# Moving the filter loads and the stores from SyncE to GpSimd, and four engines to written order, in an attention

## The chip, the cores and the metric

The kernel runs on one core of one Trainium2 chip. The metric is the device time of one execution in microseconds, the median of several runs. One further execution is recorded by the hardware profiler; its page and its trace are what the text below reads. The engines are TensorE (PE in the profile, PEld for its weight loads), VectorE (DVE), ScalarE (ACT), GpSimd (POOL) and SyncE (SP; SPq is the queue of transfers that it issues). Each engine works through its own list of instructions in order and waits on semaphores for the others.

## The reference

The input is an image batch of 2 x 128 channels x 64 x 64. Layer 0 is a convolution-attention block (a group norm, 7 x 7 neighbourhood attention, three small matrices and normalisations) added to the image. Layer 1 sees each image as 4096 tokens of 128 numbers:

```python
t = _to_tokens(x)
t = t + _L1_attn_ref(_ln_t(t))            # global attention, one head
t = t + _L1_ffn_ref(_ln_t(t), ...)        # sum of spectral filters

# _L1_attn_ref(q): queries, keys and values are the same tokens
sim = jnp.einsum('blh,bmh->blm', q, q) * scale
sim = jnp.where(diag[None, :, :], jnp.float32(-1000000000.0), sim)
attn = jax.nn.softmax(sim, axis=-1)
return jnp.einsum('blm,bmh->blh', attn, q)

# _compute_spectral: convolutions with 16 filters, then 128 x 128 matrices
out = jnp.einsum('btkd,k,kde->bte', U_plus, s, Mpp)
out = out + jnp.einsum('btkd,k,kde->bte', U_minus, s, Mpm)
```

The last part is done for four branches, each on a leading fraction of the tokens and with its own matrices, and the branches are added with weights that a softmax over `log_weights + gumbel` gives. Since a query is also a key, `sim` is symmetric.

## The kernel before

All arithmetic is in float32. The kernel has three stretches of time: layer 0 and the making of tokens (up to about 350 us, where its last work overlaps with the first attention), the global attention of image 0 and then of image 1 (about 350 to 1310 us), and the spectral filters as convolutions by matmul (from about 1310 us to the end), which the change leaves alone.

**Attention.** `attention(b, fill)` cuts 4096 tokens into 8 chunks of 512 and walks 36 pairs (a, c) with c >= a. A pair has four steps, each for 128 queries of chunk a. In a step, `weights` multiplies a query tile with the keys of chunk c into a PSUM bank (L927, near the diagonal L936), and ScalarE takes the exponential (L932, L943). The matmuls of a pair are issued while the pair before is used. The exponentials serve twice, because of the symmetry. Once as they are: `other` (L1049) adds up what chunk a gives to chunk c, in one PSUM buffer, which VectorE adds to the sums `xa` after the fourth step (L1066, L1068). And once turned, for what chunk c gives to chunk a (`own`, L983, in `onto`). To turn them, `sent` writes the pair's 1 MB to `eb` in HBM from ScalarE's queue (L956), `moved` reads it back with the partition groups exchanged in four transfers of 256 KB from SyncE's queue (L963, two buffers `et`), and `turned` transposes blocks of 32 x 32 on VectorE (L972, two instructions). Constants say how many steps after the sending each follows: `MOVE` 3 for the reads, `TURN` 7 for the transposes, `DELAY` 8 for the matmuls. `pass_on(2)` issues what has come due, at most two `own` products in a step.

**Fill.** After each step `fill()` advances generators, one piece of other work at a time. Urgent ones come first. `after(b, c)` takes a chunk that is complete: transposes (L1088), division by the softmax's sum (VectorE, L1091 to L1100), a layer norm (statistics L183, L184 on VectorE, the power -1/2 L174 on GpSimd, `z` L191 on VectorE), its transposes (L202) and copy (L1113), and short transforms of the tokens as matmuls (L1142, L1155). Their results are copied by ScalarE (`uo`, L1120), added and subtracted by `adder[0]`, which is GpSimd during the attentions (`ub`, L1123), and stored to `us` in HBM by SyncE (L1127, and in halves of 64 rows L1132). Behind the urgent ones stand, in attention 0, `filters()` (transforms of the spectral filters: matmuls L1325, sums on GpSimd L1337, L1348, stores of rows to `gs` by SyncE, L1312) and `tokens(1)`, the normalised tokens of image 1. In attention 1 there is `for_ffn`: `filter_matrices` mixes the 2 x 16 matrices of four branches in 8 groups of four (`mixed`: a load of 256 KB by SyncE, L1256, into the pool `st`, then GpSimd L1259, or L1263 and L1264), and after each pair of groups makes scaled sums and differences (L1276 to L1281); then blocks of convolution filters are loaded (`ct`, L1424).

**Order.** The instructions go to the engines through a scheduler, which may move an instruction ahead of others of its engine, except those marked `keep_in_program_order`: the reads in `moved` (L963), the transposes in `turned` (L972) and the matmuls in `onto` (L983) keep their order. Semaphores and buffers are worked out from the resulting order.

Of the kernel before, what the change touches and what calls it, by code (L numbers as in the profile page):

```python
# [24 lines left out]
MOVE, TURN, DELAY = 3, 7, 8  # L25
# [77 lines left out]
def kernel(  # L103
# [773 lines left out]
    with ap_:  # L877
# [24 lines left out]
        def attention(b, fill):  # L902
# [78 lines left out]
            def onto(own, n, out_, e, first, last):  # L981
                tc.keep_in_program_order(
                    nc.tensor.matmul(out_, lhsT=tok[b][:, n, :], rhs=e, start=first, stop=last, skip_group_check=True)  # L983
                )
# [22 lines left out]
            coming_, late, turns, owns = [], [], [], {}  # L1007
# [22 lines left out]

            es, halves = [], []
            for k in range(4):
                es.append(weights(0, 0, k, es, halves))
            for i, (a, c) in enumerate(pairs):
# [6 lines left out]
                for j in range(4):  # L1041
                    if following:
                        coming.append(coming_of(*following, j, coming, halves))
                    n = 4 * CHUNKS[a] + j
                    turn = lambda v, o: v.rearrange(o, q=4) if far(a, c) else v
                    if a == c:
# [11 lines left out]
                    pass_on(2)  # L1058
# [15 lines left out]
            complete(7, owns[7])  # L1074


        spare = [tok[0][:, 0:4, :]]
        adder = [nc.gpsimd]

        def after(b, c):  # L1080
# [35 lines left out]
            def store(pu, n, r0, m, ri):  # L1116

                for s in range(2):
# [5 lines left out]
                    for sgn in range(2):  # L1124
                        to = us[r0 : r0 + m, sgn, :, 2 * hh + s, 2 * fp : 2 * fp + 2, b, par, :]
                        if ri is not None:
                            nc.sync.dma_start(  # L1127
# [3 lines left out]
                        for f in range(2):  # L1131
                            nc.sync.dma_start(  # L1132
# [73 lines left out]
        def branch_weights():  # L1206
# [40 lines left out]
            for _ in mixed(mu, m_u, nc.vector, False):  # L1247
                pass
            yield

        def mixed(dst, src, eng, steps):
            dst2 = dst.rearrange("p k e -> p (k e)")
            for i in range(NBR):
                st = sp.tile([P, 4, P], F32, tag="st", name="st")
                n = src.shape[1]
                nc.sync.dma_start(out=st[:, 0:n], in_=src[i].rearrange("k d e -> d k e"))  # L1256
                st2 = st[:, 0:n].rearrange("p k e -> p (k e)")
                if i == 0:
                    eng.tensor_scalar(dst2, st2, wt[:, 0:1], None, ALU.mult)  # L1259
                elif eng is nc.vector:  # L1260
                    eng.scalar_tensor_tensor(dst2, st2, wt[:, i : i + 1], dst2, ALU.mult, ALU.add)
                else:
                    eng.tensor_scalar(st2, st2, wt[:, i : i + 1], None, ALU.mult)  # L1263
                    eng.tensor_tensor(dst2, dst2, st2, ALU.add)  # L1264
# [549 lines left out]
```

## Time and profile before

| what | value |
|---|---|
| time, median of 3 runs (lowest to highest) | 2090.71 us (2090.48 to 2095.21) |
| the profiled execution's own time | 2097.21 us |
| its span, first to last instruction | 2095.5 us |
| mean granted TensorE clock | 0.963 |
| TensorE busy | 1931.1 us (92%) |
| VectorE, ScalarE, GpSimd busy | 910.3, 723.4, 682.4 us |
| SyncE's reads of turned weights, `et` | 216 of 256 KB |
| SyncE's stores `us` from `ub`, of 128 KB | 128 |

The profile's page gives busy times, a picture of the span in 40 equal slices (a digit is the busy share in tenths, 52.4 us a slice), the chain of work that ended last, and groups of instructions by line, with their mean duration, the idle time of the engine just ahead of them and what ended it. Beyond the page, the trace answers for a window: the busy time of every engine, an engine's instructions in order of time, or what it waited for. A name such as `own L983 <- DVE et L972` reads: the instruction of line 983 that writes `own` waited for VectorE's instruction of line 972 that wrote `et`. Where lines of different kernels are named, they are lines of that kernel's own file.

### The profile page before, as it was taken

What the parts mean: (1) busy time and instruction counts of PE and PEld (TensorE: products, weight loads), DVE (VectorE), ACT (ScalarE), POOL (GpSimd) and SP (SyncE); (2) the same over time, 40 slices, a digit from 0 to 9 for tenths busy, and PEclk for the clock granted to TensorE, in tenths of its full rate; (3) what the DMA queues carried; (4) which work ended last, traced back from release to release, by engine and by line L of the source; (5) the groups of instructions that cost most, each with busy time, mean ns of one, the idle gap of its engine ahead of it and who ended that gap; (6) DMA issues with size and microseconds to landing.
All of it is one profiled execution on the core that took longest, in us unless ns stands there. A gap on an engine that the chain in (4) does not pass through costs nothing.

```text
span 2095.5 us, 51013 instructions
## 1 busy us (share of the span) xinstructions
PE 1931.1 (92%) x20504; PEld 1357.0 (65%) x20504; DVE 910.3 (43%) x2874; ACT 723.4 (35%) x1686; POOL 682.4 (33%) x1054
## 2 busy tenths in 40 slices
PE   6899998998899999995388998999999999999998
PEld 4677775444444444442133444699999899999987
DVE  5799986543433343422123335333333334333332
ACT  3789885313222234121022232222222222222222
POOL 4367976243011123028751111022222112222211
PEclk8999999999999999998689998999999999999999
DMA  4222222676466536466356641322222123222211
GB/s 150 62 61 61 62 60 65 199 184 187 137 191 180 164 86 214 122 184 171 101 155 167 185 134 52 87 67 66 68 66 64 46 58 100 66 70 67 66 45 42
DMA packets 278379, 225.98 MB, mean 108 GB/s; under 512 B 122607, under 2 KB 241535, under 8 KB 270720
## 3 DMA queue, kind: packets, MB, share of 16 engines
q1 hardware_dynamic: 269442, 162.59, 31.2%
q10 hardware_dynamic: 8126, 58.04, 7.0%
q8 instruction: 163, 2.67, 0.5%
q0 software_dynamic: 576, 2.10, 0.3%
q14 instruction: 72, 0.59, 0.1%
HBM read 131.40 MB, written 91.25 MB: 106 GB/s over the span
## 4 chain that ended last, share of the span: by engine, by line
PE 63%; issue 11%; POOL 9%; DMA 7%; DVE 6%; SPq 2%; ACT 1%; POOLq 0%; DVEq 0%; ACTq 0%
PE acc L1542 27%; PE pc L1523 7%; PE own L983 6%; PE bank L927 5%; PE other L1049 5%; PE bank L349 2%; PE bank L559 2%; POOL ub L1123 2%; PE bank L202 1%; POOL st L1263 1%; DMA et<-eb 1%; DMA st<-in_m_plus_dram 1%; DMA us<-ub 1%; PE bank L1142 1%; DMA st<-in_m_minus_dram 1%
## 5 line engine op out<-in xcount | busy, mean ns | idle before, releaser
L1528 DVE COPY y<-pc 128x512 f32<-128x512 f32 x320 | 206.1, 686 | 349.2 <-PE pc L1523 349.0
L1542 PE MATMUL acc<-y,mpl 32*128 32x256 f32 x5120 | 324.3, 379 | 0.8 <-DVE af L1552 0.8
L1542 PE MATMUL acc<-y,mmi 32*128 32x256 f32 x5120 | 316.5, 375 | 0.0
L1528 ACT COPY y<-pc 128x512 f32<-128x512 f32 x320 | 171.9, 589 | 397.5 <-PE pc L1523 392.9
L1542 PEld LDWEIGHTS acc<-y,mpl 32*128 32x128 f32 x5120 | 289.4, 186 | 8.0 <-DVE af L1552 1.3
L1542 PEld LDWEIGHTS acc<-y,mmi 32*128 32x128 f32 x5120 | 290.9, 185 | 3.9
L983 PE MATMUL own<-et,tok 128*128 128x512 f32 x448 | 217.3, 622 | 62.6 <-DVE et L972 60.8
L932 ACT ACTIVATE e<-bank 128x512 f32<-128x512 f32 x216 | 128.8, 599 | 406.7 <-PE bank L927 394.8
L1553 POOL TENSOR_TENSOR af<-af 128x512 f32<-128x512 f32 x39 | 49.7, 1274 | 591.8 <-DVE af L1552 540.2
L927 PE MATMUL bank<-cm 128*128 128x512 f32 x432 | 225.2, 612 | 4.5 <-ACT uo L1120 4.5
L1049 PE MATMUL other<-e,tok 128*128 128x512 f32 x448 | 225.2, 599 | 4.2 <-DVE xa L1066 4.2
L1523 PE MATMUL pc<-ct,ut 32*128 32x256 f32 x2560 | 214.5, 380 | 3.9 <-DMA ut<-us 2.1
L983 PEld LDWEIGHTS own<-et,tok 128*128 128x128 f32 x448 | 86.2, 199 | 175.4 <-issue 94.3
L1523 PEld LDWEIGHTS pc<-ct,ut 32*128 32x128 f32 x2560 | 174.4, 188 | 10.4 <-DVE y L1528 3.9
L972 DVE STREAM_TRANSPOSE et<-et 128x1024 f32<-128x1024 f32 x108 | 127.7, 1219 | 105.1 <-DMA et<-eb 105.1
L174 POOL TENSOR_TENSOR ln_rs<-ln_rs,mhalf 128x4 f32<-128x4 f32 x24 | 24.4, 1017 | 404.9 <-DVE ln_rs L173 404.9
L1049 PEld LDWEIGHTS other<-e,tok 128*128 128x128 f32 x448 | 82.8, 192 | 103.1 <-issue 95.4
L1123 POOL TENSOR_TENSOR ub<-uo 128x256 f32<-128x256 f32 (+1 forms) x164 | 99.8, 641 | 100.5 <-ACT uo L1120 69.5
L927 PEld LDWEIGHTS bank<-cm 128*128 128x128 f32 x432 | 76.7, 195 | 76.8 <-issue 62.1
L546 ACT ACTIVATE p<-p,mn 128x196 f32<-128x196 f32 x256 | 114.4, 449 | 14.1 <-DVE mn L536 13.6
L1066 DVE TENSOR_TENSOR xa<-other,xa 128x512 f32<-128x512 f32 x42 | 28.9, 687 | 167.9 <-PE other L1049 167.7
L536 DVE CUSTOM_DVE_ANT_0 p<-bank,tab 128x196 f32<-128x196 f32 x256 | 76.4, 353 | 4.9 <-PE bank L523 4.7
(262 smaller groups left out, 2607.1 us busy)
## 6 DMA issues: line engine op xcount, KB each, us to landing
eb<-e ACTq DMA_DIRECT2D x54, 1024.0 KB
et<-eb SPq DMA_DIRECT2D x216, 256.0 KB
ut<-us SPq DMA_DIRECT2D x160, 128.0 KB
us<-ub SPq DMA_DIRECT2D x128, 128.0 KB
ct<-gs SPq DMA_DIRECT2D x320, 40.0 KB
vw<-vd SPq DMA_DIRECT2D x256, 49.0 KB
ct<-gs SPq DMA_DIRECT2D x320, 32.0 KB
vd<-v SPq DMA_DIRECT2D x128, 32.0 KB
```

What stands on the lines that cost most here:

```text
L536: nc.vector.tensor_tensor_reduce(t[name + "p"][:, h, :], t[name + "S"][h][:, 0:KEYS], tab[:, ci, h, :], 1.0, 3.0e38, ALU.add, ALU.min, t[n ...
L546: nc.scalar.activation(p, p, AF.Exp, bias=t[name + "mn"][:, h : h + 1], scale=-1.0, accum_out=t["den"][:, u, h : h + 1],)
L927: nc.tensor.matmul(ps.rearrange("p (q t j) -> p q t j", q=4, t=4), lhsT=cm[b][:, n * P : (n + 1) * P], rhs=keys.rearrange("p (t q j) -> p ...
L932: nc.scalar.activation(e, ps.rearrange("p (q r) -> p q r", q=4), AF.Exp, bias=0.0, scale=ASCALE)
L972: tc.keep_in_program_order(nc.vector.transpose(flat, flat))
L983: nc.tensor.matmul(out_, lhsT=tok[b][:, n, :], rhs=e, start=first, stop=last, skip_group_check=True)
L1049: nc.tensor.matmul(turn(other, "p (q r) -> p q r"), lhsT=tok[b][:, n, :], rhs=es[j], start=(j == 0), stop=(j == 3),)
L1123: adder[0].tensor_tensor(ub[:, sgn, 0:n], both[:, 0:n], both[:, n : 2 * n], op)
L1523: nc.tensor.matmul(pcs[j].rearrange("p (g o c) -> p o g c", g=4, o=2)[:, :, at], lhsT=ut[rows_, par, :], rhs=cv_[rows_], start=True, stop= ...
L1528: (nc.scalar.copy if j % 2 else nc.vector.tensor_copy)(y[:, :, :, 4 * kl + j, :], pcs[j].rearrange("p (g x k) -> p k g x", g=4, k=KF))
L1542: nc.tensor.matmul(acc[j][:, 0:256], lhsT=(mmi if l else mpl)[rows_, k, :], rhs=y[rows_, k, 2 * l : 2 * l + 2].rearrange("p s n x -> p (s ...
L1553: eng.tensor_tensor(af[:, 0:2], af[:, 0:2], af[:, 2:4], ALU.add)
```

## The change

The change has two halves. Transfers: the loads of the branch matrices in `filter_matrices`, the stores of filter rows to `gs` and the stores of token transforms to `us` are issued by GpSimd in place of SyncE, the last until attention 1 has ended (`adder` gets a second entry for that). The loads come through a new function `branch`, one branch ahead of its mixing, and a fill now carries one branch rather than two, with the sums and differences in a fill of their own; the small matrices `mu` are mixed by VectorE as before and loaded by SyncE. `filters` hands over after every row of sums, not every second. What SyncE issues in the attentions is then the reads `et`, filter blocks `ct` and a few constants.

Order: from the step of attention 0 at which the buffer for image 1's tokens exists (`tt[1]`), and in all of attention 1, until each attention's end, a `manual_schedule` takes TensorE, VectorE, ScalarE and GpSimd out of the scheduler's hands: they run in the order in which the program writes them. SyncE stays with the scheduler. `onto` no longer has its own mark. `MOVE` goes from 3 to 2. At a pair's first step `pass_on(2)` comes ahead of the product `other`, at the other steps behind it as before. In attention 1 a `fill()` follows each of the first four weight products.

```diff
--- before.py
+++ after.py
@@ -22,7 +22,7 @@
 KF = 16
 NBR = 4
 MASKED = -1.0e30
-MOVE, TURN, DELAY = 3, 7, 8
+MOVE, TURN, DELAY = 2, 7, 8
 
 DIAG = -1.0e6
 QSCALE = DH ** -0.5
@@ -979,9 +979,7 @@
                 nc.vector.tensor_copy(et[:, m], pt)
 
             def onto(own, n, out_, e, first, last):
-                tc.keep_in_program_order(
-                    nc.tensor.matmul(out_, lhsT=tok[b][:, n, :], rhs=e, start=first, stop=last, skip_group_check=True)
-                )
+                nc.tensor.matmul(out_, lhsT=tok[b][:, n, :], rhs=e, start=first, stop=last, skip_group_check=True)
 
             def complete(a, own):
                 xs = xa[b][:, chunk(a)]
@@ -1004,7 +1002,7 @@
                 if (c, t) == (7, 3):
                     complete(a, own)
 
-            coming_, late, turns, owns = [], [], [], {}
+            coming_, late, turns, ordered, owns = [], [], [], [], {}
             step = 0
 
             def coming_of(a, c, k, left, halves):
@@ -1028,9 +1026,12 @@
                     pair_onto(owns[a], a, c, et, t)
                     n -= 1
 
+            written = ExitStack()
             es, halves = [], []
             for k in range(4):
                 es.append(weights(0, 0, k, es, halves))
+                if b:
+                    fill()
             for i, (a, c) in enumerate(pairs):
                 following = pairs[i + 1] if i + 1 < len(pairs) else None
                 coming, halves = [], []
@@ -1039,10 +1040,14 @@
                 else:
                     owns[a] = ps_o.tile([P, 512], F32, tag="own", name="own", bufs=2)
                 for j in range(4):
+                    if tt[1] is not None and not ordered:
+                        ordered.append(written.enter_context(tc.manual_schedule(engines={engines.PE, engines.DVE, engines.Activation, engines.Pool})))
                     if following:
                         coming.append(coming_of(*following, j, coming, halves))
                     n = 4 * CHUNKS[a] + j
                     turn = lambda v, o: v.rearrange(o, q=4) if far(a, c) else v
+                    if j == 0:
+                        pass_on(2)
                     if a == c:
                         onto(owns[a], n, owns[a], es[j], j == 0, a == 7 and j == 3)
                     else:
@@ -1055,7 +1060,8 @@
                             here = ep.tile([P, 4, 512], F32, tag="et", name="et", bufs=2)
                         turned_here(here, es, j)
                         late.append((step + 1, a, c, here, j))
-                    pass_on(2)
+                    if j:
+                        pass_on(2)
                     fill()
                     step += 1
                 if a != c:
@@ -1072,10 +1078,11 @@
                 pass_on(2)
                 fill()
             complete(7, owns[7])
+            written.close()
 
 
         spare = [tok[0][:, 0:4, :]]
-        adder = [nc.gpsimd]
+        adder = [nc.gpsimd, nc.gpsimd]
 
         def after(b, c):
 
@@ -1124,12 +1131,12 @@
                     for sgn in range(2):
                         to = us[r0 : r0 + m, sgn, :, 2 * hh + s, 2 * fp : 2 * fp + 2, b, par, :]
                         if ri is not None:
-                            nc.sync.dma_start(
+                            adder[1].dma_start(
                                 out=to[:, ri], in_=ub[:, sgn, :].rearrange("p (f d) -> p f d", d=P)
                             )
                             continue
                         for f in range(2):
-                            nc.sync.dma_start(
+                            adder[1].dma_start(
                                 out=to[:, :, f].rearrange("k i d -> i k d"), in_=ub[64 * f : 64 * f + 64, sgn, 0:P]
                             )
 
@@ -1244,33 +1251,37 @@
             nc.vector.tensor_tensor(wt, wt, ys, ALU.add)
 
             yield
-            for _ in mixed(mu, m_u, nc.vector, False):
-                pass
-            yield
-
-        def mixed(dst, src, eng, steps):
-            dst2 = dst.rearrange("p k e -> p (k e)")
+            mu2 = mu.rearrange("p k e -> p (k e)")
             for i in range(NBR):
-                st = sp.tile([P, 4, P], F32, tag="st", name="st")
-                n = src.shape[1]
-                nc.sync.dma_start(out=st[:, 0:n], in_=src[i].rearrange("k d e -> d k e"))
-                st2 = st[:, 0:n].rearrange("p k e -> p (k e)")
+                st = branch(m_u, i, nc.sync)
                 if i == 0:
-                    eng.tensor_scalar(dst2, st2, wt[:, 0:1], None, ALU.mult)
-                elif eng is nc.vector:
-                    eng.scalar_tensor_tensor(dst2, st2, wt[:, i : i + 1], dst2, ALU.mult, ALU.add)
+                    nc.vector.tensor_scalar(mu2, st, wt[:, 0:1], None, ALU.mult)
                 else:
-                    eng.tensor_scalar(st2, st2, wt[:, i : i + 1], None, ALU.mult)
-                    eng.tensor_tensor(dst2, dst2, st2, ALU.add)
-                if i % 2 and steps:
-                    yield
+                    nc.vector.scalar_tensor_tensor(mu2, st, wt[:, i : i + 1], mu2, ALU.mult, ALU.add)
+            yield
+
+        def branch(src, i, eng):
+
+            st = sp.tile([P, 4, P], F32, tag="st", name="st")[:, 0 : src.shape[1]]
+            eng.dma_start(out=st, in_=src[i].rearrange("k d e -> d k e"))
+            return st.rearrange("p k e -> p (k e)")
 
         def filter_matrices(mpl, mmi):
 
-            for k0 in range(0, KF, 4):
-                for dst, src in ((mpl, m_plus), (mmi, m_minus)):
-                    yield from mixed(dst[:, k0 : k0 + 4, :], src[:, k0 : k0 + 4], nc.gpsimd, True)
-
+            parts_ = [(k0, dst, src, i) for k0 in range(0, KF, 4) for dst, src in ((mpl, m_plus), (mmi, m_minus)) for i in range(NBR)]
+            loaded = [branch(m_plus[:, 0:4], 0, nc.gpsimd)]
+            for at, (k0, dst, src, i) in enumerate(parts_):
+                if at + 1 < len(parts_):
+                    k1, _, src1, i1 = parts_[at + 1]
+                    loaded.append(branch(src1[:, k1 : k1 + 4], i1, nc.gpsimd))
+                st = loaded.pop(0)
+                dst2 = dst[:, k0 : k0 + 4].rearrange("p k e -> p (k e)")
+                nc.gpsimd.tensor_scalar(dst2 if i == 0 else st, st, wt[:, i : i + 1], None, ALU.mult)
+                if i:
+                    nc.gpsimd.tensor_tensor(dst2, dst2, st, ALU.add)
+                yield
+                if dst is mpl or i + 1 < NBR:
+                    continue
                 a, d = (m[:, k0 : k0 + 4, :].rearrange("p k e -> p (k e)") for m in (mpl, mmi))
                 s = sp.tile([P, 512], F32, tag="st", name="mdiff")
                 nc.gpsimd.tensor_tensor(s, a, d, ALU.subtract)
@@ -1309,7 +1320,7 @@
                     gs.tensor, gs.offset + r0 * 4 * SG * GROW + (i * SG + s) * GROW + o * LL,
                     [[4 * SG * GROW, n], [2 * SG * GROW, 2], [1, LL]],
                 )
-                nc.sync.dma_start(out=to, in_=src)
+                nc.gpsimd.dma_start(out=to, in_=src)
 
             everything = [(r0, c0 + ri * P, (ri,), P) for r0, c0 in row_tiles for ri in range(2)]
             everything.append((left_row, left_col, (0, 1), 64))
@@ -1347,8 +1358,7 @@
                         fn = sp.tile([P, 2, LL], F32, tag="ub", name="fn", bufs=4)
                         nc.gpsimd.tensor_scalar(fn[mine], fb[mine], -1.0, None, ALU.mult)
                         store(fn[mine], r0, n, 1, s, 1, 0)
-                    if a == 1:
-                        yield
+                    yield
 
         def residual_of(lags):
             for _ in range(4):
@@ -1462,7 +1472,7 @@
         kept = []
         fill, left = filler(1, steps, kept)
         attention(1, fill)
-        adder[0] = nc.vector
+        adder[:] = nc.vector, nc.sync
         for gen in steps:
             for _ in gen:
                 pass
```

More of the change, by code (lines that the diff above doesn't have):

```diff
@@ L1246, in branch_weights @@
             yield
-            for _ in mixed(mu, m_u, nc.vector, False):
-                pass
-            yield
-        def mixed(dst, src, eng, steps):
-            dst2 = dst.rearrange("p k e -> p (k e)")
-            for i in range(NBR):
-                st = sp.tile([P, 4, P], F32, tag="st", name="st")
-                n = src.shape[1]
-                nc.sync.dma_start(out=st[:, 0:n], in_=src[i].rearrange("k d e -> d k e"))
-                st2 = st[:, 0:n].rearrange("p k e -> p (k e)")
-                if i == 0:
-                    eng.tensor_scalar(dst2, st2, wt[:, 0:1], None, ALU.mult)
-                elif eng is nc.vector:
-                    eng.scalar_tensor_tensor(dst2, st2, wt[:, i : i + 1], dst2, ALU.mult, ALU.add)
-                else:
-                    eng.tensor_scalar(st2, st2, wt[:, i : i + 1], None, ALU.mult)
-                    eng.tensor_tensor(dst2, dst2, st2, ALU.add)
-                if i % 2 and steps:
-                    yield
@@ L1268, in filter_matrices @@
-        def filter_matrices(mpl, mmi):
-            for k0 in range(0, KF, 4):
-                for dst, src in ((mpl, m_plus), (mmi, m_minus)):
-                    yield from mixed(dst[:, k0 : k0 + 4, :], src[:, k0 : k0 + 4], nc.gpsimd, True)
+            mu2 = mu.rearrange("p k e -> p (k e)")
+            for i in range(NBR):
+                st = branch(m_u, i, nc.sync)
+                if i == 0:
+                    nc.vector.tensor_scalar(mu2, st, wt[:, 0:1], None, ALU.mult)
+                else:
+                    nc.vector.scalar_tensor_tensor(mu2, st, wt[:, i : i + 1], mu2, ALU.mult, ALU.add)
```

## The prediction

> **What bounds the kernel now.** I read the page's slices first, to see where the time has a shape, then the windows over the odd slices, then the timelines of TensorE (PE) and of SyncE's queue (SPq) inside them.
>
> ```profile
> span 2095.5 us, 51013 instructions
> PE   6899998998899999995388998999999999999998
> POOL 4367976243011123028751111022222112222211
> PEclk8999999999999999998689998999999999999999
> ```
>
> A slice is 52.4 us. TensorE is the bound at nine tenths nearly everywhere; the hole is slices 18 and 19 (943 to 1048 us), where GpSimd (POOL) is the busy one and the granted clock falls too. Windows of 105 us around it (columns: busy time of PE, PEld, DVE, ACT, POOL, then clock, DMA share, GB/s):
>
> ```profile
> 840.00:945.00 105.00, 104.09 (x280) 46.40 (x279) 35.07 (x83) 23.23 (x41) 11.89 (x17) 1.00 0.55 156
> 945.00:1050.00 105.00, 43.98 (x98) 18.56 (x96) 19.27 (x39) 7.72 (x14) 86.91 (x76) 0.73 0.48 132
> 1050.00:1155.00 105.00, 87.94 (x249) 38.77 (x250) 28.70 (x53) 24.19 (x44) 33.62 (x43) 0.89 0.58 161
> ```
>
> So the attention runs without a gap before, and loses most of a window while GpSimd mixes filter matrices. TensorE's timeline says on what (start, duration, instruction, in brackets idle before it and its releaser):
>
> ```profile
> 968.79 3.70 PE L983 MATMUL own<-et,tok 128*128 128x512 f32 x8 [0.23 <-DVE et L972]
> 999.42 5.90 PE L983 MATMUL own<-et,tok 128*128 128x512 f32 x8 [26.92 <-DVE et L972]
> 1025.04 6.74 PE L983 MATMUL own<-et,tok 128*128 128x512 f32 x8 [19.72 <-DVE et L972]
> 1053.19 0.45 PE L202 MATMUL bank<-ident,z 128*128 128x128 f32 x1 [15.68 <-DVE z L191]
> ```
>
> The turned weights come late, and the same eight matmuls take 5.90 and 6.74 us after a wait instead of 3.70. SyncE's queue in that stretch explains why:
>
> ```profile
> 1015.99 4.36 SPq L1256 DMA_DIRECT2D st<-in_m_minus_dram  x2
> 1029.13 15.46 SPq L1256 DMA_DIRECT2D st<-in_m_plus_dram  x4
> 1047.10 9.38 SPq L1256 DMA_DIRECT2D st<-in_m_minus_dram  x4
> 1056.57 13.49 SPq L963 DMA_DIRECT2D et<-eb  x8
> ```
>
> The reads of turned weights (L963) stand behind filter loads (L1256) that wait for a buffer of GpSimd, four of which took 15.46 us to get through. That is the wait the change removes. GpSimd's own work, by form:
>
> ```profile
> L1123 POOL TENSOR_TENSOR ub<-uo 128x256 f32<-128x256 f32 x112 | 77.7, 727 | 73.0 <-ACT uo L1120 62.5 <-DMA et<-eb 8.9 <-DMA us<-ub 1.6
> L1263 POOL TENSOR_SCALAR st<-st,wt 128x512 f32<-128x512 f32 x24 | 37.7, 1569 | 34.7 <-DMA st<-in_m_plus_dram 24.6 <-DMA st<-in_m_minus_dram 9.6 <-issue 0.2
> L174 POOL TENSOR_TENSOR ln_rs<-ln_rs,mhalf 128x4 f32<-128x4 f32 x24 | 24.4, 1017 | 404.9 <-DVE ln_rs L173 404.9
> L1264 POOL TENSOR_TENSOR mpl<-mpl,st 128x512 f32<-128x512 f32 x12 | 15.1, 1262 | 1.0
> ```
>
> (busy time, mean ns of one, idle before it.) The 121 us of mixing are spread over 936 to 1072 us, with 34.7 us of idle for loads; L174, the power in a normalisation, idles for its input; only the 15.68 us above come from it, standing behind mixing that the scheduler had put ahead.
>
> **What the Trainium skill says.** "DMA: Bandwidth & Descriptors", section "SWDGE vs HWDGE vs iDMA": descriptors of a DMA issued by GpSimd are computed in software on GpSimd's own cores; so each one is work in that engine's line. Its section "Anatomy of one DMA — SWDGE (gpsimd) path" says "You can emit a lot of descriptors before the incremental cost shows up", which is for a low price. The trace of before has one such place, four transfers of 128 rows of 4 KB:
>
> ```profile
> 19.35 2.51 POOL L802 DMA_DIRECT2D xa<-in_x_dram  x4
> ```
>
> 0.63 us each, and GpSimd's next operation starts at 21.88: the issue holds up the line. "SBUF — State Buffer", in its box on DVE blocking such DMAs and the text on it, gives some 620 ns for one alone (agrees) and some 3100 ns beside a VectorE copy that takes the shared port (nothing here shows it). "TensorE: Matmul & The Clock Gate", Part 1: after idling the array runs at half clock for some microseconds; 5.90 and 6.74 against 3.70 us agree.
>
> **The change part by part.** *What moves.* GpSimd gets 280 more DMAs (32 filter loads, 32 stores of filters' Toeplitz rows, the rest token stores: per normalisation 8 large of 256 runs, 8 small of 64 rows); SyncE loses them. And PE, DVE, ACT and POOL now run in the written order from the first normalised tokens of attention 0 to the end of each attention, where before a scheduler chose it. So a late GpSimd reaches TensorE. The path: the next normalisation's power (L174) is written behind all earlier mixing, loads and stores; VectorE's z (L191) waits for it; the evacuation of the product "other" (L1066) is written behind z; "other" has one buffer, so TensorE's next product into it waits.
>
> *Prices.* A pair of matmuls of 128x512 takes 0.857 us back to back (x8, so four pairs, in 3.43), twelve pairs make four steps: 2.57 us a step. The unknown is GpSimd's time per DMA. Low end, in line with the skill's sentence: 0.59 (L802's three 537 to 588 ns; the fourth 808) whatever the runs, 0.54 for small ones. High end, in proportion to runs: loads of 512 runs 2.36, stores of 256 runs 1.18. I take 0.8 for large stores, 0.55 for small, 1.1 for loads, since four times the runs should show in part but not in full. To a load I add 0.5 for its landing: one is issued ahead, under 2.8 us of mixing, and in the chain of waits landings took 2.6 to 3.3 us, some 7 to 9.
>
> 1. *Mixing, attention 1.* One normalisation's copies and stores: 8 x 0.727 + 4 x 0.456 = 7.6 (L1123), and 8 x 0.8 + 8 x 0.55 = 10.8 of issue: 18.4. The built order has 18 branches and two difference steps before the next power. A branch is 1.57 (L1263) and, three times in four, 1.26 (L1264): 2.52. A difference step is 2 x 1.265 + 8 x 0.607 = 7.39. So 18.4 + 45.4 + 14.8 + loads 18 x 1.6 + 1.1 = 29.9 + 1.5 for power and a copy = 110, with lead-in, z and evacuation 113.8. TensorE has 26 steps and 2.4 of the normalisation to do: 69.2. Stall 44.6. To the power after that, 14 branches: 18.4 + 35.3 + 14.8 + 20.8 + 1 = 90.3 against 24 steps + 4.1 = 65.8: 24.5. With 6 for matmuls at half clock 75 lost. Before, the same 47 steps took 221.6 us (910.96 to 1132.59) where 47 x 2.57 + 6.9 = 127.7 is work: 93.9 lost. **-19** (low end 39 lost, -55; high 106, +12).
> 2. *Filters' rows, attention 0* (435 to 485 us): GpSimd 24 x 0.727 + 8 x 1.485 (L1337, L1348) + 16 x 0.8 + 16 x 0.55 + 18.4 + two powers 2.0, lead-in 3.8 = 75 against 20.5 steps + 10.1 = 62.8: 12, and 3 of half clock; before shows 9.6 idle, 11 with its slow matmuls. **+4** (-3 to +12).
> 3. *From attention 0 to 1* three normalisations follow closely: GpSimd 18.4 + 4.1 = 22.5 against 12.2 of TensorE, then 17.9 against 13.3, 5 of half clock: 20; before lost 2. **+18** (+13 to +24).
> 4. *Turned weights* are late no more, as nothing that waits stands before their reads: the stall at 557 us goes (4.7, and eight matmuls at 6.72 for 3.60). **-8.**
> 5. *Written order in eight normalisations*: VectorE's chain of transposed rows 2.5, statistics 1.9, power 1.0, z 4 x 0.348, evacuation 0.69 is 7.5, against seven pairs, 6.0. 8 x 1.5: **+12**; the residual tokens' chains likewise **+3**, both estimates.
> 6. *At nothing*: MOVE 3 to 2 (reads start 2.57 us earlier and five steps, 13 us, before their transposes; TensorE hides them, and without that cover they cost their landing of some 5 us per pair); coefficient loads of the residual filters on SyncE, as before; first weights of attention 1 with a fill after each, under TensorE's work; the last token stores. The convolution from 1310 us is TensorE's and untouched.
>
> Sum: -19 + 4 + 18 - 8 + 12 + 3 = **+10** on the profiled execution of 2097.21 us (span 2095.5), which lies 6.5 above the median; I move the median by the same, 2090.7 + 10 = **2101**. All low ends together -38, all high ends +55.
>
> **Rivals.** (A) *Faster.* A load's issue takes about 0.6 us whatever its runs and lands under the mixing: -38 to -15, some 2066. For it: 0.63 us measured, the skill's sentence. Against: L802 has a quarter of a load's runs. It decides below a load's price (issue and landing) of 1.28 us, since 31 loads x 0.32 make up the +10. (B) *Clearly slower.* The price goes by runs, +40 to +55, some 2138. For it: the page's software queue shows 576 packets for four transfers, 144 each, so a load has hundreds. Against: issuing occupied 0.6 us only. (C) *Cancels*: SyncE's wait is replaced by GpSimd's at the same length, within 6 us, 2091; for it, the mixing's 121 us and its place are unchanged. That the change doesn't do what it says is no rival: the built order shows loads and stores in GpSimd's line, and SyncE with turned weights and convolution filters alone.
>
> **How the numbers follow.** 0.3% is 6.3 us, what a measurement of this kernel can about tell from no change. Chances: middling price, +6 to +28, 0.35; (B) beyond that 0.18; (A) 0.32; (C) 0.15. So faster 0.32, same 0.15, slower 0.53. Range 2066 to 2138: from the middle of A's to the near end of B's, leaving one in ten on either side; the likeliest's own is 2097 to 2118.
>
> **What would show it.** GpSimd's DMA instructions, loads at L1266 and stores at L1134, L1139 and L1323: their mean is the disputed price. TensorE: no wait worth naming for turned weights, but two of 25 to 45 us before the "other" product (L1054) or L202 in the mixing, behind z L191 and the power; some 10 us at the attentions' boundary; 1 to 2 us at each normalisation. L174 no longer idles for VectorE there. The prediction is wrong if loads issue in 0.6 us (2066), if landings beside the weights' traffic reach 7 us each (B), or if TensorE has more work before the dependent product than the steps I counted.

## The result, and the profile after

The changed kernel takes 2142.96 us (median of 4 runs, 2138.15 to 2148.75), the kernel before 2091.60 beside it: a ratio of 1.0244, 95% interval 1.0214 to 1.0273, 51 us slower. The forecast was 2101 with a range to 2138. The direction was right; the size was not, and the time lies above the range. The profiled execution took 2138.15 us, 41 more than that of before.

The page's slices of the changed kernel (53.4 us each):

```profile
span 2136.4 us, 50841 instructions
PE   6899998977999998999094998799999999999998
POOL 3377876257133356227886345022222122222211
PEclk8999999988999998999596999899999999999999
```

The old hole has become two, a slice with 0 tenths and one with 4 for TensorE (slices 19 and 21, counted from 0), and there are smaller dents at slices 8 and 9. Windows of 105 us (PE, PEld, DVE, ACT, POOL busy, clock, DMA share, GB/s):

```profile
860.00:965.00 105.00, 101.66 (x279) 46.07 (x278) 33.61 (x80) 25.15 (x45) 23.05 (x38) 0.98 0.54 153
965.00:1070.00 105.00, 54.43 (x134) 24.27 (x133) 22.87 (x44) 11.90 (x21) 84.20 (x84) 0.77 0.58 163
1070.00:1175.00 105.00, 72.47 (x204) 32.69 (x203) 24.46 (x49) 19.68 (x35) 75.87 (x84) 0.83 0.55 146
```

What TensorE waits for, in the table of waits from 335 to 1350 us (total us, times, longest):

```profile
PE other L1054 <- DVE xa L1072: 115.4, 11, 49.0
PE bank L202 <- DVE z L191: 14.9, 3, 6.5
PE bank L949 <- ACT e L943: 13.8, 4, 7.5
PE own L982 <- DVE et L972: 4.3, 7, 1.0
```

In the kernel before, the same table from 335 to 1335 us reads:

```profile
PE own L983 <- DVE et L972: 60.8, 12, 26.9
PE bank L202 <- DVE z L191: 30.6, 6, 15.7
PE other L1049 <- DVE xa L1066: 4.2, 5, 0.9
```

The waits for turned weights, 60.8 us before, are down to 4.3. In their place stands the product `other`, which waits for its evacuation. Its two long waits on TensorE's timeline, and VectorE's timeline at the first:

```profile
1068.14 2.08 PE L1054 MATMUL other<-e,tok 128*128 128x512 f32 x2 [48.99 <-DVE xa L1072]
...
1165.61 2.07 PE L1054 MATMUL other<-e,tok 128*128 128x512 f32 x2 [31.50 <-DVE xa L1072]
```

```profile
1018.81 0.17 DVE L173 TENSOR_SCALAR ln_rs<-ln_mv 128x4 f32<-128x4 f32 x1
1065.55 1.94 DVE L191 TENSOR_SCALAR z<-tt,ln_mv,ln_rs 128x128 f32<-128x128 f32 x4 [46.56 <-POOL ln_rs L174]
1067.41 0.68 DVE L1072 TENSOR_TENSOR xa<-other,xa 128x512 f32<-128x512 f32 x1
```

This is the path that the prediction named: VectorE has the variance at 1018.8 and stands until the power (L174) at 1065.5, because the evacuation (L1072) is written behind z. GpSimd's timeline shows why the power is late, and by form what issuing cost:

```profile
1058.06 0.79 POOL L1266 DMA_DIRECT2D st<-in_m_plus_dram  x1 [0.29 <-POOL mmi L1292]
1058.89 1.57 POOL L1279 TENSOR_SCALAR mpl<-st,wt 128x512 f32<-128x512 f32 x1
1060.76 0.79 POOL L1266 DMA_DIRECT2D st<-in_m_plus_dram  x1 [0.30 <-POOL mpl L1279]
1061.59 1.57 POOL L1279 TENSOR_SCALAR st<-st,wt 128x512 f32<-128x512 f32 x1
1063.24 1.26 POOL L1281 TENSOR_TENSOR mpl<-mpl,st 128x512 f32<-128x512 f32 x1
1064.46 1.05 POOL L174 TENSOR_TENSOR ln_rs<-ln_rs,mhalf 128x4 f32<-128x4 f32 x1
```

```profile
L1134 POOL DMA_DIRECT2D us<-ub x112 | 81.9, 732 | 0.0
L1139 POOL DMA_DIRECT2D us<-ub x104 | 69.3, 671 | 3.0 <-issue 2.1 <-POOL ub L1130 0.8
L1323 POOL DMA_DIRECT2D gs<-fb x24 | 14.8, 638 | 3.6 <-POOL fb L1348 3.6
L1266 POOL DMA_DIRECT2D st<-in_m_minus_dram x16 | 12.7, 795 | 4.4 <-POOL mpl L1281 2.1 <-POOL mmi L1279 1.2 <-POOL mmi L1281 1.2
```

The disputed price is known: 0.73 us for a large store, 0.67 for a small one, 0.64 for a filter row, 0.80 for a load. A load has eight times the runs of a small store and costs a fifth more. So rival (B) is out as a mechanism, though its time came nearest.

To see where the 41 us arose I set the starts of the same product in both traces beside each other (each pair's first `other`; for the end, the convolution's first matmul). Attention 0, to its last such product: 393.9 us before, 416.1 after, +22.2. From there over the boundary to the tenth pair of attention 1: 162.5 and 184.4, +22.0. The rest of attention 1, with the mixing: 406.5 and 407.5, +0.9. The start of attention 0 came 4.0 us earlier after the change, which the change does not explain: over all kernels below it lies between 357 and 363 us. Each stage is read from one profiled execution, so a few microseconds of it mean little.

### The profile page after: what moved, and what is told of

It reads as the page before. It is cut to its first block, busy times and chain, and to the rows that moved or that the text cites. A ratio compares the mean times of both kernels' runs of the same rounds, so it can differ in the third digit from the quotient of the medians.

```text
span 2136.4 us, 50841 instructions
## 1 busy us (share of the span) xinstructions
PE 1925.9 (90%) x20504; PEld 1356.3 (63%) x20504; DVE 920.4 (43%) x2874; ACT 723.1 (34%) x1686; POOL 876.3 (41%) x1334
## 4 chain that ended last, share of the span: by engine, by line
PE 68%; POOL 13%; DVE 8%; issue 5%; DMA 4%; ACT 2%; SPq 1%; DVEq 0%; POOLq 0%; ACTq 0%
PE acc L1552 26%; PE own L982 8%; PE pc L1533 7%; PE other L1054 6%; PE bank L927 6%; PE bank L349 2%; PE bank L936 1%; POOL st L1279 1%; PE bank L202 1%; PE bank L559 1%; POOL ub L1130 1%; PE bank L1149 1%; DMA st<-in_m_minus_dram 1%; ACT p L546 1%; POOL us L1134 1%
## 5 line engine op out<-in xcount | busy, mean ns | idle before, releaser
L1054 PE MATMUL other<-e,tok 128*128 128x512 f32 x448 | 241.8, 622 | 117.7 <-DVE xa L1072 115.4
L927 PE MATMUL bank<-cm 128*128 128x512 f32 x432 | 229.6, 614 | 0.0
L982 PEld LDWEIGHTS own<-et,tok 128*128 128x128 f32 x448 | 84.2, 192 | 121.1 <-issue 100.3
L174 POOL TENSOR_TENSOR ln_rs<-ln_rs,mhalf 128x4 f32<-128x4 f32 x24 | 24.7, 1030 | 248.9 <-DVE ln_rs L173 248.8
L1127 ACT COPY uo<-bank 128x512 f32<-128x512 f32 (+1 forms) x96 | 47.0, 516 | 122.1 <-PE bank L1149 54.8
L1134 POOL DMA_DIRECT2D us<-ub x112 | 81.9, 732 | 0.0
```

The costliest lines, as they stand in the source:

```text
L927: nc.tensor.matmul(ps.rearrange("p (q t j) -> p q t j", q=4, t=4), lhsT=cm[b][:, n * P : (n + 1) * P], rhs=keys.rearrange("p (t q j) -> p ...
L1054: nc.tensor.matmul(turn(other, "p (q r) -> p q r"), lhsT=tok[b][:, n, :], rhs=es[j], start=(j == 0), stop=(j == 3),)
L1134: adder[1].dma_start(out=to[:, ri], in_=ub[:, sgn, :].rearrange("p (f d) -> p f d", d=P))
```

## The experiments

Theory 1 is that of the prediction: GpSimd's line is overfull in places, and the written order carries its lateness to TensorE. Rival 2: a DMA on GpSimd is dear in itself. Rival 3: the written order alone costs the time. I first took the two halves apart.

**Transfers only.** The edit takes the changed kernel and puts `MOVE`, the mark in `onto`, the order of `pass_on` and the fills of the first weights back, and drops the manual schedule (two of its places are shown). The mixing keeps its new hand-over of one branch a fill:

```diff
-MOVE, TURN, DELAY = 2, 7, 8
+MOVE, TURN, DELAY = 3, 7, 8
...
-                    if tt[1] is not None and not ordered:
-                        ordered.append(written.enter_context(tc.manual_schedule(...)))
```

> Only the transfers move to GpSimd (loads one branch ahead, one branch a fill); the scheduler orders the engines as before, MOVE is 3. Theory 1 (GpSimd's line is overfull in the mixing, and the written order makes every late GpSimd result reach TensorE): the mixing still blocks the next power, so its stall stays near 80 us as before, but filters' rows, attention boundary and the normalisations lose their extra 40 us: about 2092 us. Rival 2 (issuing on GpSimd is dear in itself, wherever): stays near 2140.

Measured: 2106.50 us (2104.91 to 2108.98), ratio 1.0057 [1.0038, 1.0077]. TensorE's timeline has one stall in the mixing:

```profile
1074.21 1.33 PE L202 MATMUL bank<-ident,z 128*128 128x128 f32 x4 [90.88 <-DVE z L191]
```

The scheduler had put the power behind 28 of the 32 branches in GpSimd's line and three difference steps, as in the kernel before, and now behind 29 loads and 16 stores as well. So GpSimd's line is the stall here too, 90.9 us in one piece; from 930 to 1180 us the kernel before idled 78 us in all, in three long waits and some short ones. The extra of attention 0 and of the boundary is gone: the tenth pair of attention 1 starts within 3 us of before. Theory 1 holds, at 14 us more than its number; rival 2 is out.

**Order only.** Loads and stores go back to SyncE, all else stays as changed:

```diff
-        adder = [nc.gpsimd, nc.gpsimd]
+        adder = [nc.gpsimd, nc.sync]
...
-            loaded = [branch(m_plus[:, 0:4], 0, nc.gpsimd)]
+            loaded = [branch(m_plus[:, 0:4], 0, nc.sync)]
...
-                    loaded.append(branch(src1[:, k1 : k1 + 4], i1, nc.gpsimd))
+                    loaded.append(branch(src1[:, k1 : k1 + 4], i1, nc.sync))
...
-                nc.gpsimd.dma_start(out=to, in_=src)
+                nc.sync.dma_start(out=to, in_=src)
```

> Written order, MOVE 2 and all else as in the changed kernel, but loads and stores are issued by SyncE again. Theory 1: GpSimd's line loses 31 loads of 1.1 us and some 11 us of stores for each normalisation, so the two stalls of 49 and 31.5 us shrink by about 55 us together, if turned weights' reads aren't late again behind them: 2090, with late reads 2110. Rival 3 (the written order alone costs it, not GpSimd's load): stays above 2130.

Measured: 2114.43 us, ratio 1.0096 [1.0075, 1.0117]: the branch with late reads. Two of TensorE's waits in it:

```profile
1022.90 3.40 PE L982 MATMUL own<-et,tok 128*128 128x512 f32 x4 [5.38 <-DVE et L972]
...
1048.41 2.08 PE L1054 MATMUL other<-e,tok 128*128 128x512 f32 x2 [12.23 <-DVE xa L1072]
```

The stalls of 49 and 31.5 are 12.2 and 5.9, and eleven waits of 2 to 6 us for turned weights are back. Each half alone costs less (13 and 21 us against the kernel before beside it) than both together (51), so rival 3, the written order as the whole cause, is out: it is 21 of 51. By stage, in us, from the profiled execution of each:

| stage | before | transfers only | order only | both |
|---|---|---|---|---|
| attention 0 | 393.9 | 389.5 | 420.1 | 416.1 |
| boundary, to the tenth pair | 162.5 | 165.1 | 172.4 | 184.4 |
| rest of attention 1 | 406.5 | 420.0 | 384.7 | 407.5 |

The stages do not have one cause. In attention 0 the written order alone costs all of it, 26 us, whoever issues the transfers. At the boundary the halves cost 3 and 10 us alone and 22 together. In the rest the transfers alone cost 14, the order alone gains 22 (both with the new hand-over of one branch a fill), and together nothing is gained: there the moved transfers fill the line that the written order makes everyone wait for.

**Which transfers.** Loads alone back on SyncE, and in another kernel the stores alone (the lines are those of the last diff, divided):

```diff
-                    loaded.append(branch(src1[:, k1 : k1 + 4], i1, nc.gpsimd))
+                    loaded.append(branch(src1[:, k1 : k1 + 4], i1, nc.sync))
```

> The changed kernel with the filter loads alone back on SyncE. Theory 1 (the stalls are the length of GpSimd's line): the line of the mixing loses 31 issues of 0.8 us and their gaps of 0.3, 34 us, so the two stalls of 49 and 31.5 fall to some 45 together; -34 us at most, about 2113, less gained if turned weights' reads stand behind waiting loads again (5 us each time). Attention 0 unchanged. If the landings and not the issues make the line long, the stalls stay above 65.

```diff
-        adder = [nc.gpsimd, nc.gpsimd]
+        adder = [nc.gpsimd, nc.sync]
-                nc.gpsimd.dma_start(out=to, in_=src)
+                nc.sync.dma_start(out=to, in_=src)
```

> The changed kernel with both kinds of stores alone back on SyncE. Theory 1: filters' rows lose 32 issues of 0.64 us with gaps of 0.3, so the waits of 3.7 and 13.1 us in attention 0 go; each normalisation loses 11 us of GpSimd's line, so the two stalls of the mixing fall by some 11 each and the boundary of the attentions by some 9: -35 to -45, about 2103. The loads' share stays: two stalls of about 38 and 20 us.

In the first of these the load ahead of the loop goes to SyncE too. Measured: 2112.23 us with the loads on SyncE (ratio 1.0083 [1.0057, 1.0109]), 2126.51 with the stores on it (1.0154 [1.0127, 1.0180]). With loads on SyncE, TensorE's timeline has

```profile
1053.01 2.07 PE L1054 MATMUL other<-e,tok 128*128 128x512 f32 x2 [11.92 <-DVE xa L1072]
...
1120.41 3.74 PE L982 MATMUL own<-et,tok 128*128 128x512 f32 x4 [7.84 <-DVE et L972]
...
1141.25 2.08 PE L1054 MATMUL other<-e,tok 128*128 128x512 f32 x2 [7.22 <-DVE xa L1072]
```

The two stalls fell to 19 us together, not 45, but five late reads of 3.8 to 7.8 us, 26 in all, came back, so that the idle of both kinds is 45. GpSimd's line to the two powers is 28 us shorter (95.6 and 88.8 us, where it was 114.2 and 98.3); the loads' issues left it, but not their landings, for which GpSimd waits 27 us here and 22 in the changed kernel. The gain of 31 us is near the 34 forecast. With stores on SyncE the stalls are 36.9 and 16.5, near the 38 and 20 forecast, but not for the reason given: the line to the two powers is only 3 and 6 us shorter, and late reads of 8.0 and 7.6 us hold TensorE back ahead of the stalls. The boundary is 13 us shorter; in attention 0 the waits of 3.7 and 13.1 us shrink to 2.7 and 1.7, and yet it takes 424.1 us, 8 more, with new waits before `own` products. There are five of 5 to 8 us in all, and the gain is 16 us by medians, not 35 to 45.

**The pace of the mixing.** One more `yield` behind each branch, so that a branch has two steps of TensorE, 5.1 us, and not one:

```diff
                     nc.gpsimd.tensor_tensor(dst2, dst2, st, ALU.add)
                 yield
+                yield
```

> The changed kernel with one branch of the mixing in every second fill: 5.14 us of TensorE for each branch in place of 2.57, against some 4.0 to 4.7 us of GpSimd for it. Theory 1: both stalls of the mixing vanish but for a few us: 2143 less 70 to 80, about 2068. Rivals 2 and 3: GpSimd issues and mixes as much, in the same order, so no more than 10 us change.

Measured: 2095.40 us (20 runs, 2086.40 to 2104.32), ratio 1.0006 [0.9992, 1.0019]. What is left of the stalls:

```profile
1030.05 2.07 PE L1054 MATMUL other<-e,tok 128*128 128x512 f32 x2 [10.83 <-DVE xa L1072]
...
1103.32 2.07 PE L1054 MATMUL other<-e,tok 128*128 128x512 f32 x2 [7.15 <-DVE xa L1072]
...
1167.96 2.08 PE L1054 MATMUL other<-e,tok 128*128 128x512 f32 x2 [9.61 <-DVE xa L1072]
```

80.5 us became three waits of 27.6 together and a fourth of 3.4. The operations, the transfers and the rule of written order are the same. What has changed is how much mixing is written ahead of a power in GpSimd's line: 18 branches and two difference steps, then 14 and two, have become 10 and one, 8 and one, 7 and one, and 3. 48 us came off where 70 to 80 were expected; ahead of each of the three powers there still stand a normalisation's copies and stores and a difference step beside the branches.

**The early loads.** SyncE issues the loads of `mu` and of the filters' pieces `pn` two fills ahead of VectorE's use of them (a helper that runs the two `lags` of a half together is left out):

```diff
+            coming_in = [branch(m_u, i, nc.sync) for i in range(2)]
             for i in range(NBR):
-                st = branch(m_u, i, nc.sync)
+                yield
+                yield
+                st = coming_in.pop(0)
...
+                if i + 2 < NBR:
+                    coming_in.append(branch(m_u, i + 2, nc.sync))
...
             def lags(hh, e):
                 pn = sp.tile([P, KF, 2, LG], F32, tag="st", name="pn")
                 nc.sync.dma_start(...)
+                yield
+                yield
                 at = (2 * hh + e) * LL
```

> The changed kernel, but the loads of the residual matrices (mu) and of the spectral filters' pieces (pn) are issued by SyncE two fills ahead of their use by VectorE, in attention 0. If the two stalls of 4.2 and 7.5 us at 432 and 443 us come from VectorE standing in its line for a transfer issued in the same fill, they go with their half-clock matmuls: -12 to -16, about 2129. If they only hand on another lateness: no change.

This looks into a stall that the prediction did not have. In the changed kernel TensorE's and VectorE's timelines read:

```profile
432.48 0.47 PE L949 MATMUL bank<-ident,e 128*128 128x128 f32 x1 [4.21 <-ACT e L943]
...
443.00 0.48 PE L949 MATMUL bank<-ident,e 128*128 128x128 f32 x1 [7.49 <-ACT e L943]
...
529.96 2.08 PE L1054 MATMUL other<-e,tok 128*128 128x512 f32 x2 [13.07 <-DVE xa L1072]
```

```profile
430.42 1.27 DVE L1260 SCALAR_TENSOR_TENSOR mu<-st,wt,mu 128x384 f32<-128x384 f32 x2 [5.58 <-DMA st<-in_m_u_dram]
...
438.83 0.44 DVE L1309 COPY cm<-pn 128x128 f32<-128x128 f32 x2 [6.74 <-DMA pn<-in_phi_pad_dram]
441.88 0.44 DVE L1309 COPY cm<-pn 128x128 f32<-128x128 f32 x2 [2.61 <-DMA pn<-in_phi_pad_dram]
442.24 0.29 DVE L941 TENSOR_TENSOR bank<-bank,ndiag 128x128 f32<-128x128 f32 x1
```

The mixing of `mu` and the copies wait for transfers that the same fill issued, and the diagonal's mask (L941) is written behind them; the exponential, the transposes and TensorE wait for that (4.21 us at 432.48, 7.49 at 443.00). Measured: 2134.97 us (2131.73 to 2142.52), ratio 1.0197 [1.0169, 1.0226], 8 less than the changed kernel by medians. Both waits are gone, but the work behind them comes some 40 us later (the first filter product at 488.8 us and not at 448.4) and meets other evacuations: TensorE's waits of over 0.9 us from 420 to 760 us fell only from 39 to 30 us. The cause of the two waits is shown. What they are worth is less sure: the runs of the two kernels overlap (2138.15 is the lowest of the changed one), and 8 us agrees with the 9 us of idle that went, not with the 12 to 16 expected.

**Slack in the normalisation.** One more fill before `ln_apply` in `after`:

```diff
             stats = ln_statistics(kept_)
             yield True
+            yield True
             ln_apply(z, kept_, stats)
```

> The changed kernel with one more fill between a normalisation's statistics and its z. Step 5 of the prediction (in the written order z stands before the evacuation of the product, and its chain is longer than TensorE's work): the waits of 2.2 to 2.7 us at six normalisations go with their half-clock matmuls, and the two stalls of the mixing start one step later: -12 to -20, about 2127. If the waits aren't of that chain's length, they stay.

Measured: 2118.59 us, ratio 1.0116 [1.0094, 1.0139], 24 less than the changed kernel by medians. Of seven waits of 2.2 to 2.7 us behind z, counted over both attentions, one of 1.7 is left. By stage, attention 0 is 8 us shorter, the boundary, where three normalisations follow each other, 14, and the rest of attention 1 only 1: its two stalls are 3 and 4 us shorter (45.6 and 27.4), but two waits for turned weights, of 2.9 and 6.6 us, have come. Slow matmuls did not follow every wait, as the expectation had it. Two of the seven in the changed kernel:

```profile
644.38 1.12 PE L1054 MATMUL other<-e,tok 128*128 128x512 f32 x2 [2.68 <-DVE xa L1072]
...
942.83 2.07 PE L1054 MATMUL other<-e,tok 128*128 128x512 f32 x2 [2.65 <-DVE xa L1072]
```

The next pair took 1.1 us after three of them and 1.4 to 2.1 after four; 1.02 is usual.

**MOVE.** The changed kernel with the old distance of the reads:

```diff
-MOVE, TURN, DELAY = 2, 7, 8
+MOVE, TURN, DELAY = 3, 7, 8
```

> The changed kernel with MOVE 3 again: turned weights are read one step, 2.57 us, later. Step 6 of the prediction puts it at nothing: within 4 of 2143. If the transfers are only just in time beside the filter loads, waits for turned weights appear: 2150 or more.

Measured: 2143.52 us, ratio 1.0242 [1.0227, 1.0257]: nothing, as expected.

**The kernel before, paced.** If pace decides, the old kernel has the same cure with no transfer moved. It handed out two branches a fill; this edit gives it the pace of the kernel above, one branch in every second fill, a quarter of its own:

```diff
-                if i % 2 and steps:
+                if steps:
+                    yield
                     yield
```

> The kernel before, whose only edit is the pace of the mixing: one branch in every second fill in place of two in each fill; SyncE issues all as before. Theory 1 in its general form (GpSimd is given 2.5 us of mixing and a landing in less time of TensorE than that, whoever issues the loads): most of the 94 us lost there go, with 20 left: about 2020. If the loads in SyncE's line are the cause whatever the pace, no more than 20 us come off: above 2070.

Measured: 2042.63 us (2041.64 to 2047.38), ratio 0.9759 [0.9735, 0.9783], faster than both kernels. Of the 78 us that TensorE idled from 930 to 1180 us, 31 are left, 20 of them in three waits:

```profile
992.70 0.45 PE L202 MATMUL bank<-ident,z 128*128 128x128 f32 x1 [8.04 <-DVE z L191]
...
1069.27 0.45 PE L202 MATMUL bank<-ident,z 128*128 128x128 f32 x1 [8.37 <-DVE z L191]
...
1133.66 0.45 PE L202 MATMUL bank<-ident,z 128*128 128x128 f32 x1 [3.67 <-DVE z L191]
```

and none over 3.0 us before an `own` product (that is, for turned weights) in the mixing. Ahead of the first of these powers stand 9 branches and one difference step where 28 and three stood. The loads in SyncE's line (L1256) waited 40.3 us for GpSimd there, where they waited 69.5 before, so they hold up less behind them. The rest of attention 1, with the mixing, takes 356.7 us, and 357.2 in the changed kernel at the same pace. A difference step of 7.4 us still stands ahead of each of these powers, so I cut it in three fills and gave a group's first branch, a single operation, one fill (the edit against the last kernel):

```diff
                     yield
-                    yield
+                    if i:
+                        yield
...
                 nc.gpsimd.tensor_tensor(a, a, d, ALU.add)
+                yield
                 for k in range(4):
+                    if k == 2:
+                        yield
```

> The kernel before with the mixing paced: two fills for a branch (one for a group's first, which is a single operation), and the sums and differences cut in three fills. The waits of 8.0, 8.4 and 3.7 us that the half pace left stand behind sums and differences of 7.4 us and a branch: they should fall to some 3 each, 2043 - 10 = about 2032. If they are of another length, 2043.

Measured: 2027.55 us (2024.64 to 2033.05), ratio 0.9690 [0.9672, 0.9709], the fastest kernel of all, 15 us below the last where 10 were expected. The three waits are 1.6, 3.2 and 2.5 us.

**All paces in the written order, and who issues.** The changed kernel with half the pace of mixing, early loads, slack, and one more fill after each filter row with a negated copy; and the same with loads and stores on SyncE. Beyond the edits shown:

```diff
                         store(fn[mine], r0, n, 1, s, 1, 0)
+                        yield
                     yield
```

> The changed kernel with four paces at once: a branch in every second fill, the early loads in attention 0, one more fill between statistics and z, and one more fill after each filter row that needs a negated copy. If the causes are separate, the gains add: 48 + 8 + 24 and some 14 for the row stage, 2143 - 94 = 2049; if the stalls only stand in for one another, above 2075.

> The same four paces and the written order, but loads and stores issued by SyncE. If it matters who issues (turned weights' reads wait behind loads and stores in SyncE's line, five waits of 5 us and their half clock), it is 15 to 30 slower than the paced kernel with GpSimd's issues; if pace alone decides, within 6 of it; if GpSimd's own issues still cost the path something, faster.

Measured: 2039.13 us with GpSimd's issues (ratio 0.9735 [0.9707, 0.9763]) and 2039.44 with SyncE's (0.9744 [0.9730, 0.9759]). The gains add, to 104 us where 94 were expected. And the two are the same. One line of each, the windows of the former's mixing and a wait in the latter:

```profile
965.00:1070.00 105.00, 96.63 (x257) 42.71 (x258) 37.85 (x78) 25.55 (x45) 84.02 (x91) 0.97 0.73 199
```

```profile
1042.29 3.78 PE L982 MATMUL own<-et,tok 128*128 128x512 f32 x4 [7.75 <-DVE et L972]
```

GpSimd is as busy as in the changed kernel's window (84.0 against 84.2 us), yet TensorE works 96.6 us of 105 and not 54.4. With SyncE issuing, four waits of 7 to 10 us for turned weights remain; with GpSimd issuing, three of 3 to 5 us, and more waits of 1 to 7 us of other kinds. In the sum the two kernels come out the same. Neither is faster than the kernel before with its mixing paced (2027.55 us), so no run here shows a gain from the change itself.

## Why the prediction was wrong

The likeliest case was the right one in kind: the waits for turned weights are replaced by waits behind GpSimd's line, on the path named (power, z, evacuation, product), with issue prices near those taken. Two terms of its sum failed. It had +10 us on the profiled execution, and 41 were measured. By stage: attention 0 was put at +5 (steps 2 and 4, half of 5, the residual tokens) and cost 22.2; the boundary was put at +18 and cost 22.0; the rest of attention 1 was put at -13 (step 1 and half of 5) and came to +0.9; the other -4.0 is the earlier start. So 17 of the 31 us missed lie in attention 0 and 14 in the mixing; the boundary's 4 and the start's -4 cancel.

- *Step 2, +4, failed most.* The wait behind GpSimd's line came as worked out, 13.1 us (at 530 us) against 12. What is missing stands ahead of it: 4.2 and 7.5 us (at 432 and 443) behind the loads of `mu` and `pn`, and 3.7 (at 477) behind a z that took 2.5 us where 1.1 is usual. That makes 28.4 us of idle where 12 were worked out and 9.6 were lost before. Step 6 put coefficient loads on SyncE at nothing, "as before", and I did not ask what is queued behind VectorE's wait for them. In the kernel before VectorE waits 6.8 us for `pn` too, but TensorE idles only 3.3 us for it; in the written order all that stands behind the wait is late with it. Taking the two waits away gave 8 us by medians. Nor is GpSimd's line what makes attention 0 long: with loads and stores on SyncE in the same order the 13.1 us become 1.7, late reads come in their place, and attention 0 takes 420.1 us all the same.
- *Step 1, -19, was too hopeful by 14.* The counts of branches ahead of each power were right, 18 and 14. Stalls of 44.6 and 24.5 were worked out, 49.0 and 31.5 are there. GpSimd's line to the first power is 114.2 us (951.33 to 1065.51) against 110; to the second 98.3 from power to power against 90.3, of which 3.7 was a wait for the next normalisation's first product, not counted. Over the pairs of the mixing the gain was 4.7 us (227.7 to 223.0), not 19. Half the pace took off 48 us, which shows that the amount of mixing ahead of a power sets this stretch.
- *Prices.* 0.8, 0.55 and 1.1 us taken for large stores, small stores and loads; 0.73, 0.67 and 0.80 measured. A load also has a gap of 0.29 behind the mixing operation ahead of it, and the mixing waited 22 us in all for 32 landings, 0.7 each: 1.8 with the issue, where 1.6 was taken. That is some 6 us over 31 loads, a part of step 1's miss.
- *Step 3, +18.* Measured 22; the mechanism is GpSimd's copies and stores and the slow z together, as the runs with stores on SyncE (13 off) and with slack (14 off) show.
- *Step 4, -8.* The waits for turned weights did go. With the transfers moved alone, attention 0 was 4.4 us shorter, in one profile of each.
- *Step 5, +12.* The mechanism was right. Seven waits of 2.2 to 2.7 us, 18 in all, are in the trace where eight of 1.5, 12 in all, were counted. Slack took 8 us off attention 0, where half of the term was 6; the larger part of its 24 us belongs to step 3.
- *Step 6, MOVE at nothing*: right, 2143.52 against 2142.96.
- *From the profile to the median* I moved both by the same. The profiled execution of before was slower than its timed runs and that of after as fast as its fastest, which accounts for 10 us of the 42 by which 2101 missed.
- *The range.* Its upper end, 2138, is the middle of (B); the near end, as the prediction calls it, would be 2131.

What stays open: how the remaining difference in attention 0 divides between single waits, since removing one moves the next.

## What to carry over

When one engine does background work beside another that bounds the kernel, compare the two per hand-over: here 4 to 5 us of GpSimd were handed out for 2.6 us of TensorE, and in the one pair of kernels that tested it, which engine issued the transfers made no difference once the pace was right. Where an order is fixed by hand, every wait in it is a wait for all that is written behind it, so go through each engine's waits for transfers too, not only through the work that the change moves: the order alone cost attention 0 26 us. A wait that disappears from a profile is worth only what the next one behind it leaves.

## What was unexpected of the hardware

In the changed kernel the issue of a transfer by GpSimd occupied its line for 0.51 to 0.84 us over all forms, from stores of filter rows to loads of 512 runs of 512 bytes. Small stores of 64 rows took 0.67 us in the mean and the loads 0.80, so the price is not in proportion to the runs. Where the operation just ahead of it in GpSimd's line was one that it depends on, the issue stood another 0.29 us, at loads and filter rows; the large stores, which have another operation in between, show no such gap. VectorE's work beside it hardly lengthened an issue: loads took 0.80 us beside it and 0.79 without, large stores 0.74 and 0.73.

The Trainium skill's page "SBUF — State Buffer", in its section "A bandwidth-pool intuition that's wrong (but worth ruling out)", has ~620 ns for a DMA issued by GpSimd alone and ~3100 ns beside a VectorE copy. The run with early loads has three large stores issued beside VectorE's copies from `pn` to `cm`, both in SBUF: the issues took 0.85, 0.73 and 0.73 us where 0.72 is usual. Three of the four copies there grew instead, to 0.80, 0.80 and 1.24 us where 0.26 is usual; since GpSimd also adds between the issues, what held them is open. The page's ~3100 ns is not seen, but these copies are short, and an issue is not the whole of a DMA: in the changed kernel the large stores took a median of 3.7 us from issue to landing. So the prediction's "agrees", too, sets 0.63 us of an issue beside what the page gives for a DMA.
